# Layer 3 of the last batch: unpacked sign weights, one output per product, and the check of the sums moved ahead of its second half

## Chip, cores and metric

The kernel runs on one core of one Trainium2 chip. The metric is the device time of one execution in microseconds (us); lower is better. Times inside an execution are given from the start of the profiled span.

## What is computed

The input is `x`, 8 batches of 512 channels and 1024 (32 x 32) positions, in f32. Four layers follow each other:

- layer 0: three 1x1 convolutions to 64 channels, a batch norm over all batches for two of them, an attention without softmax that is divided by the largest singular value, a 1x1 convolution back to 512 channels, and a residual;
- layer 1: a group norm, an attention over 1024 positions with 512 channels and softmax, a projection, and a residual;
- layer 2: an attention over 1024 positions with 128 channels and softmax, a projection to 512 channels with a scale (`bn`), and a residual;
- layer 3, which the change touches:

```python
a = jnp.sign(x + c(rsign_bias))
scale = jnp.mean(jnp.abs(W), axis=1)
Wb = jnp.sign(W) * scale[:, None]
y = jnp.einsum('bchw,oc->bohw', a, Wb)
bn = c(bn_gamma) * (y - c(bn_mean)) * jax.lax.rsqrt(c(bn_var) + BN_EPS) + c(bn_beta)
s = bn + x
t = s - c(pr_shift)
out = jnp.where(t > 0, t, c(pr_slope) * t) + c(pr_bias)
```

Its product has only signs on both sides, so every sum of it is a whole number of at most 512 in size.

## The kernel before, in words

**Stages.** An opening stage loads the weights and all batches once, makes layer 0's projections and statistics, and folds weight products together. After it the main stage calls `fast` (line 768) once for each batch, in the order 6, 7, 0, 1, 2, 3, 4, 5. A last part reads one number, `bad`, and computes everything again on a general path if it isn't zero (lines 1444 and 1445). In the runs shown it is zero, so that path is skipped by a branch.

**One batch in `fast`.** The scores of layer 1 (`scores1`) and its values (`make_v`, `values1`, line 519) are block products of the Strassen kind: seven products where eight would be usual, with sums and differences of the blocks on VectorE. Then come layer 2's projections (`project2`, line 611), its scores (`scores2`), and its values (`values2`, L826). The 1024 positions are two halves of 512. Each half of layer 2 is closed by `close2` (line 646): four f32 products with the weights `z` (L650), added to the batch `xt` on VectorE (L652). An f32 product of 128x512 is two passes of TensorE in the trace. In the batches before the last, parts of the next batch's work (`make_u`, `split_h`) fill the gaps.

**Layer 3** is `leave` (line 654), a generator that does one half of the positions. ScalarE makes the signs of `xt` in f16 (L660, four instructions of 128x512, one per block of 128 channels). The sign weights lie packed in `sw3` (128 x 4 x 256, f16): one number holds two output channels, `lo + 1026 * hi`. A loop over `j` (0 and 1) makes four f16 products (L666) that accumulate into one PSUM bank; this bank holds two outputs' sums at once. They are taken apart in three steps: ScalarE divides by 1026 and adds a large constant, which rounds (L675); VectorE subtracts that constant (L676), which gives the upper sum; VectorE subtracts 1026 times the upper sum from the bank (L677), which gives the lower. For each of the two outputs of 128 channels there follow five more steps: a scale and the addition of `xt` on VectorE (L680), Relu (L684) and Identity (L685) on ScalarE, their combination on VectorE (L692), and the output transfer on SP's queue (L695).

**Where the halves of layer 3 stand.** The first half of a batch is done inside `fast` between the two `close2`. The second half is put on a list, `rest3`, and is done step by step beside the next batch's scores. The last batch has no next one, so its second half follows at once (lines 856 to 859) and with nothing beside it.

**The check of the sums.** For each batch and each attention `inverse_sums` (line 727) writes a few of the inverse softmax sums to the tile `guard` (64 rows x 2 x 128) by SP's queue (L745). After the last batch, nine small VectorE instructions (L1319 to L1329) see whether any is too large, too small, or differs too much between the halves. A product of one element on TensorE (L1331) counts the rows that fail, and VectorE copies the count to `bad` (L1332). `values_load` (L1444) then loads `bad` into a register on all five engines, and each engine branches on it (L1445). The end of the program (L1498) is a barrier of all engines.

**What sets the order.** The program is traced, and outside of a few hand-ordered TensorE passages of the opening stage a scheduler puts the instructions of each engine in order; waits between engines are semaphores. The order that the text speaks of is that of the built programs. Eight PSUM banks rotate under `bank` (line 121); the tiles `h`, `hs`, `us`, `uv` of the pool `big` have one buffer each, `small` has three, `e` eight.

Of the kernel before, what the change touches and what calls it, by code (L numbers as in the profile page):

```python
# [20 lines left out]
CC = C // P  # L21
# [62 lines left out]
def kernel(  # L84
# [36 lines left out]
    def bank():  # L121
        return psum["bank"].tile([P, HF], F32, tag="bank", name="bank")
# [16 lines left out]
    def half(i):  # L139
        return bass.ts(i, HF)  # L140
# [510 lines left out]
            xs = xt[:, oc, half(h)]  # L651
            nc.vector.tensor_tensor(xs, ps, xs, ALU.add)  # L652

    def leave(env, xt, dst, halves=range(NH)):

        small = env["small"]
        for h in halves:
            sg = env["e"].tile([P, CC, HF], F16, tag="e", name="sg")
            for cc in range(CC):
                nc.scalar.activation(  # L660
                    sg[:, cc, :], xt[:, cc, half(h)], AF.Sign, bias=rb3[:, cc : cc + 1]
                )
            for j in range(CC // 2):
                ps = bank()
                for cc in range(CC):
                    mm(  # L666
                        out=ps,
                        lhsT=sw3[:, cc, bass.ts(j, P)],
                        rhs=sg[:, cc, :],
                        start=cc == 0,  # L670
                        stop=cc == CC - 1,
                    )
                both = env["e"].tile([P, 2, HF], F32, tag="e", name="both")
                y1, y2 = both[:, 0, :], both[:, 1, :]
                nc.scalar.activation(y2, ps, AF.Identity, bias=round3, scale=1.0 / PACK)  # L675
                nc.vector.tensor_scalar(y2, y2, ROUND, None, ALU.subtract)  # L676
                nc.vector.scalar_tensor_tensor(y1, y2, -PACK, ps, ALU.mult, ALU.add)  # L677

                for y, oc in ((y1, j), (y2, j + 2)):
                    nc.vector.scalar_tensor_tensor(  # L680
                        y, y, sa3[:, oc : oc + 1], xt[:, oc, half(h)], ALU.mult, ALU.add
                    )
                    up = small.tile([P, HF], F32, tag="half_a", name="up3")
                    nc.scalar.activation(up, y, AF.Relu, bias=cb3[:, oc : oc + 1])  # L684
                    nc.scalar.activation(  # L685
                        y,
                        y,
                        AF.Identity,
                        bias=pb3[:, oc : oc + 1],
                        scale=col("L3_conv_pr_slope", oc),  # L690
                    )
# [4 lines left out]
                yield  # L696

    def channels(ap):
        return ap.rearrange("(cc p) n -> p cc n", p=P)
# [64 lines left out]
        return steps()  # L764

    rest3 = []

    def fast(env, n, hb, ua):
# [12 lines left out]

        es = [None] * NT
        for k, _ in enumerate(scores1(env, hb, ua, es)):
            if rest3 and k % 2:
                if next(rest3[0], "end") == "end":
                    rest3.pop()
                    if more and order[n + 1] not in resident:
                        resident[order[n + 1]] = load_x(order[n + 1])
            if k == 8 and more:
                ahead = entering(n + 1)  # L790
            if k >= 11 and k % 3 == 0:
                next(ahead, None)
# [12 lines left out]
        steps = iter(())  # L805
        for k, _ in enumerate(values1(env, xt, vt, es, r, scratch)):
            chore(2)
            if k == 5 and more:
                nxt = resident[order[n + 1]]
                hb = split_h(env, normal(env, nxt))  # L810
        if more:
            steps = make_u(env, hb, got)

        def fill(k=1):
            for _ in range(k):
                next(steps, None)

        tt, pt, gt = project2(env, xt, lambda h: fill(1 - h))
        es, esum = scores2(env, pt, tt, lambda t: fill(t % 2))
        banks, r = [None, None], None  # L820

        def values2(h, ts):
            if banks[h] is None:
                banks[h] = bank()
            for t in ts:
                mm(  # L826
                    out=banks[h],
                    lhsT=gt[:, t, :],
                    rhs=es[t][:, half(h)],
                    start=t == 0,  # L830
                    stop=t == NT - 1,
                )
# [14 lines left out]
        close2(xt, att, 0)  # L847
        att = values2(1, range(NTH, NT))
        fill()
        for _ in leave(env, xt, dst, [0]):  # L850
            fill()
        close2(xt, att, 1)
        fill(2)
        for _ in steps:
            pass
        rest3.append(leave(env, xt, dst, [1]))
        if not more:
            for _ in rest3.pop():
                pass

        return hb, got[0] if more else None
# [437 lines left out]
    with ExitStack() as main:  # L1299
        psum_pools(main, 0, 8)  # L1300
        big = main.enter_context(tc.tile_pool(name="big", bufs=1, reuse_waits="tile"))
        epool = main.enter_context(tc.tile_pool(name="epool", bufs=EBUFS))
        small = main.enter_context(tc.tile_pool(name="small", bufs=3))
        env.update({"big": big, "e": epool, "small": small})
        got = []
        hb = split_h(env, normal(env, resident[order[0]], True))
        for _ in make_u(env, hb, got):
            pass
        ua = got[0]
        for n in range(B):  # L1310
            hb, ua = fast(env, n, hb, ua)

        g = 2 * B * 4
        fine = small.tile([g, NH, P], F32, tag="half_a", name="fine")
        other = small.tile([g, NH, P], F32, tag="half_b", name="other")
        nbad = small.tile([g, 1], F32, tag="nbad", name="nbad")
        nc.vector.tensor_scalar(fine, guard, 1.0 / GUARD, None, ALU.is_gt)  # L1319
        nc.vector.tensor_scalar(other, guard, GUARD, None, ALU.is_lt)  # L1320
        nc.vector.tensor_tensor(fine, fine, other, ALU.mult)
        for h in range(NH):
            one = slice(0, g // 2)
            nc.vector.scalar_tensor_tensor(
                other[one, h, :], guard[one, 1 - h, :], RATIO, guard[one, h, :], ALU.mult, ALU.is_gt
            )
            nc.vector.tensor_tensor(fine[one, h, :], fine[one, h, :], other[one, h, :], ALU.mult)
        nc.vector.tensor_reduce(nbad, fine.rearrange("p h n -> p (h n)"), AX.X, ALU.min)
        nc.vector.tensor_scalar(nbad, nbad, -1.0, 1.0, ALU.mult, ALU.add)  # L1329
        ps = bank()  # L1330
        mm(out=ps[0:1, 0:1], lhsT=nbad, rhs=ones2[0:g, 0:1], start=True, stop=True)  # L1331
        nc.vector.tensor_copy(bad, ps[0:1, 0:1])  # L1332


    def attention(env, scores, scale, apply):

        at = None
# [107 lines left out]
    with tc.If(again > 0):  # L1445
        with (
            ExitStack() as stack,
            tc.tile_pool(name="gbig", bufs=1) as big,
# [53 lines left out]
```

## Time and profile before

| | us |
|---|---|
| three runs | 2003.36, 2006.15, 2007.2 |
| median | 2006.15 |
| profiled execution | 2006.29 |
| its span | 2004.5 |

The profile has five engines: PE is TensorE's matrix products, PEld its weight loads, DVE is VectorE, ACT is ScalarE, POOL is GpSimd; SP only issues transfers here. A letter q after an engine's name means its sequencer or queue. "bank<-sg,sw" means that an instruction writes `bank` from `sg` and `sw`; L666 is line 666. In the chain of work each row is a start, a length and what ran, and a row "issue" is time in which the engine waited for nothing that the profile shows.

The costliest groups of the page, with instructions, busy time and mean duration of one:

| line | engine | what | count | busy us | mean ns |
|---|---|---|---|---|---|
| L536 | PE | values of layer 1, 128x512 f32 | 768 | 334.0 | 593 |
| L369 | PE | scores of layer 1, 128x512 f32 | 384 | 183.3 | 598 |
| L826 | PE | values of layer 2, 128x512 f32 | 256 | 114.6 | 595 |
| L710 | PE | scores of layer 2, 128x512 f32 | 256 | 114.6 | 592 |

Rows of the kinds that the change touches, from the groups and from the views of single lines (128x512 unless another size is given):

| line | engine | what | ns |
|---|---|---|---|
| L666 | PE | f16 product, at full clock / at most | 379 / 634 |
| L650 | PE | f32 pass | 592 |
| L660 | ACT | signs | 717 |
| L675 | ACT | rounding step, from PSUM | 685 |
| L684, L685 | ACT | Relu, Identity | 716, 798 |
| L676 | DVE | subtraction of the constant | 423 |
| L677 | DVE | lower sum, from PSUM | 683 |
| L680, L692 | DVE | scale and add, combine | 744, 739 |
| L652 | DVE | close of layer 2, from PSUM | 679 |
| L1005 | DVE | packing of the signs, 128x1024 f16, once | 1218 |

The duration of a product is longer than its spacing: eight products of L666 stand at 1974.48 to 1976.37, one every 0.216 us.

### The profile page before, as it was taken

The numbers are of one execution on the slowest core, as the hardware profiler recorded it, in microseconds if no ns is written. First come the engines' busy times: TensorE is split into PE (matmuls) and PEld (weight loads), VectorE is DVE, ScalarE is ACT, GpSimd is POOL, SyncE is SP. The second block draws the span as 40 slices with busy tenths as digits, with TensorE's granted clock in tenths as the row PEclk, the third lists the DMA queues.
The fourth block names the chain that finished last, engine by engine and source line by source line (L and its number), as shares of the span: only waits on it lengthen the run. The fifth ranks groups of instructions, "written<-read, shape, count | busy, mean of one in ns | idle before, by whom it ended". The sixth has DMA issues, their size and how long they took to land.

```text
span 2004.5 us, 16625 instructions
## 1 busy us (share of the span) xinstructions
PE 1935.0 (97%) x6246; PEld 996.0 (50%) x6246; DVE 1113.0 (56%) x1827; ACT 539.0 (27%) x842; POOL 187.9 (9%) x152
## 2 busy tenths in 40 slices
PE   8999899999999999999999999999999999999995
PEld 2377346544465446454465446444645445544652
DVE  3245577337863586536752677248653675266435
ACT  2132222134221432124211332034202421233014
POOL 0000001100011000200011001100120011101110
PEclk9989999999999999999999999999999999999997
DMA  8320000002000020001100010002000200010001
GB/s 330 126 74 1 5 6 11 1 11 84 10 7 0 21 74 17 0 0 43 57 11 1 32 69 11 0 11 84 11 0 1 77 29 0 0 32 21 11 1 54
DMA packets 26711, 66.99 MB, mean 33 GB/s; under 512 B 3760, under 2 KB 4016, under 8 KB 25984
## 3 DMA queue, kind: packets, MB, share of 16 engines
q1 hardware_dynamic: 25968, 65.09, 9.5%
q8 instruction: 51, 0.84, 0.2%
q0 software_dynamic: 224, 0.33, 0.1%
q10 hardware_dynamic: 432, 0.43, 0.1%
q14 instruction: 36, 0.29, 0.0%
HBM read 38.51 MB, written 18.87 MB: 29 GB/s over the span
## 4 chain that ended last, share of the span: by engine, by line
PE 92%; DVE 4%; ACT 3%; issue 0%; DMA 0%; DVEq 0%; ACTq 0%
PE bank L369 36%; PE bank L536 19%; PE bank L826 6%; PE bank L621 5%; PE bank L710 5%; PE bank L1073 4%; PE bank L633 3%; PE bank L650 3%; PE bank L392 2%; PE bank L666 1%; PE bank L876 1%; PE wide L1129 1%; PE bank L1183 1%; PE bank L877 1%; PE bank L731 1%; DVE e L326 1%
## 5 line engine op out<-in xcount | busy, mean ns | idle before, releaser
L536 PE MATMUL bank<-e,vt 128*128 128x512 f32 x768 | 334.0, 593 | 0.0
L536 PEld LDWEIGHTS bank<-e,vt 128*128 128x128 f32 x768 | 145.0, 190 | 175.4 <-issue 171.7
L369 PE MATMUL bank<-ut,h 128*128 128x512 f32 x384 | 183.3, 598 | 4.7 <-ACT e L331 4.7
L369 PE MATMUL bank<-us,hs 128*128 128x512 f32 x256 | 121.3, 596 | 0.5 <-DVE us L298 0.5
L326 DVE TENSOR_TENSOR e<-bank,e 128x512 f32<-128x512 f32 x128 | 87.6, 684 | 61.3 <-PE bank L369 60.0
L826 PE MATMUL bank<-e,tpg 128*128 128x512 f32 x256 | 114.6, 595 | 0.0
L710 PE MATMUL bank<-tpg 128*128 128x512 f32 x256 | 114.6, 592 | 0.0
L369 PEld LDWEIGHTS bank<-ut,h 128*128 128x128 f32 x384 | 70.6, 190 | 87.7 <-issue 73.5
L621 PE MATMUL bank<-xt,tpg 128*128 128x512 f32 x256 | 113.6, 592 | 0.0
L369 PE MATMUL bank<-wo,h 128*128 128x256 f32 x384 | 95.7, 389 | 18.3 <-ACT vt L331 18.3
L717 ACT ACTIVATE e<-bank 128x512 f32<-128x512 f32 x128 | 76.4, 597 | 88.2 <-PE bank L710 88.2
L369 PE MATMUL bank<-h,wu 128*128 128x512 f32 x192 | 92.1, 603 | 3.4 <-DVE h L442 3.4
L326 DVE TENSOR_TENSOR vt<-bank,vt 128x512 f32<-128x512 f32 x64 | 44.0, 687 | 90.2 <-PE bank L369 89.3
L341 POOL TENSOR_TENSOR ut<-ut 128x512 f32<-128x512 f32 x16 | 21.8, 1360 | 733.9 <-ACT ut L322 733.9
L722 DVE TENSOR_TENSOR esum<-esum,e 128x1024 f32<-128x1024 f32 x48 | 58.8, 1226 | 54.8 <-ACT e L717 54.8
L369 PEld LDWEIGHTS bank<-wo,h 128*128 128x128 f32 x384 | 72.4, 193 | 31.0 <-ACT vt L331 21.5
L341 POOL TENSOR_TENSOR e<-e 128x512 f32<-128x512 f32 x32 | 41.6, 1301 | 441.1 <-ACT e L320 370.2
L826 PEld LDWEIGHTS bank<-e,tpg 128*128 128x128 f32 x256 | 48.0, 190 | 63.9 <-issue 63.9
L710 PEld LDWEIGHTS bank<-tpg 128*128 128x128 f32 x256 | 48.6, 190 | 60.8 <-issue 58.6
L621 PEld LDWEIGHTS bank<-xt,tpg 128*128 128x128 f32 x256 | 47.9, 190 | 56.4 <-issue 55.0
L369 PEld LDWEIGHTS bank<-us,hs 128*128 128x128 f32 x256 | 47.3, 190 | 57.5 <-issue 51.4
L660 ACT ACTIVATE sg<-xt,rb 128x512 f16<-128x512 f32 x64 | 43.7, 717 | 103.4 <-DVE xt L652 100.7
(300 smaller groups left out, 2995.9 us busy)
## 6 DMA issues: line engine op xcount, KB each, us to landing
xt<-in_x SPq DMA_DIRECT2D x56, 512.0 KB
out<-both SPq DMA_DIRECT2D x64, 256.0 KB
rfull<-rsum SPq DMA_DIRECT2D x64, 128.0 KB
f_dram<-f SPq DMA_DIRECT2D x8, 256.0 KB
fb<-f_dram SPq DMA_DIRECT2D x8, 256.0 KB
w<-in_w SPq DMA_DIRECT2D x1, 1024.0 KB
q<-in_w_q SPq DMA_DIRECT2D x1, 1024.0 KB
k<-in_w_k SPq DMA_DIRECT2D x1, 1024.0 KB
```

The source lines that it names most:

```text
L326: nc.vector.tensor_tensor(dst, ps, u, ALU.add)
L341: nc.gpsimd.tensor_tensor(c22, c22, c12, ALU.add)
L369: mm(out=ps[:, q * w : (q + 1) * w], lhsT=lt(ka, kb, q, k), rhs=rhs(ka, kb, q, k), start=first and q == 0 and k == 0, stop=last and k == 1 ...
L536: mm(out=ps, lhsT=a[:, t, bass.ts(r_, P)], rhs=e[t], start=first and t == 0, stop=last and t == NTH - 1, skip_group_check=True,)
L621: mm(out=ps, lhsT=sbw["tpg"][:, cc, bass.ts(i, P)], rhs=xt[:, cc, half(h)], start=cc == 0, stop=cc == CC - 1,)
L633: mm(out=ps[:, i, :], lhsT=xt[:, cc, bass.ts(4 * h + i, P)], rhs=sbw["tpg"][:, cc, 2 * P : 3 * P], start=cc == 0, stop=cc == CC - 1,)
L650: mm(out=ps, lhsT=sbw["z"][:, bass.ts(oc, P)], rhs=att, start=True, stop=True)
L710: mm(out=ps, lhsT=pt[:, 0, bass.ts(t, P)], rhs=tt[:, 0, half(h)], start=True, stop=True,)
L717: nc.scalar.activation(e[:, half(h)], ps, AF.Exp, scale=float(P) ** -0.5)
L722: nc.vector.tensor_tensor(esum, esum, e, ALU.add)
L826: mm(out=banks[h], lhsT=gt[:, t, :], rhs=es[t][:, half(h)], start=t == 0, stop=t == NT - 1,)
L1073: mm(out=banks[i][side(h), :], lhsT=w0[i][:, cc, :], rhs=xt[:, cc, half(h)], start=cc == 0, stop=cc == CC - 1,)
```

## The change

For the last batch only, `unpacked` makes two tiles of plain signs, `lo` and `hi` (f16, in the buffer of the tag `h`), out of `sw3`, with the same arithmetic that took the sums apart: three VectorE instructions of 128x1024. `leave` gets them as `signs` and then makes two products per `j`, one with `lo` and one with `hi`, each into its own bank; the three steps that took the sums apart are left out, and the scale and addition reads the bank. All other batches use `leave` as before.

The nine small instructions of the check, the product that counts, the copy to `bad` and the load of `bad` on all engines are now a function, `count_bad`, that is called after the last batch's second `close2` and before its second half of layer 3. Its three tiles come from the pool `late`, outside the main stage's pools. The branch stays at the end.

```diff
-    def leave(env, xt, dst, halves=range(NH)):
+    def leave(env, xt, dst, halves=range(NH), signs=None):
...
-                ps = bank()
-                for cc in range(CC):
-                    mm(
-                        out=ps,
-                        lhsT=sw3[:, cc, bass.ts(j, P)],
-                        rhs=sg[:, cc, :],
-                        start=cc == 0,
-                        stop=cc == CC - 1,
-                    )
                 both = env["e"].tile([P, 2, HF], F32, tag="e", name="both")
                 y1, y2 = both[:, 0, :], both[:, 1, :]
-                nc.scalar.activation(y2, ps, AF.Identity, bias=round3, scale=1.0 / PACK)
-                nc.vector.tensor_scalar(y2, y2, ROUND, None, ALU.subtract)
-                nc.vector.scalar_tensor_tensor(y1, y2, -PACK, ps, ALU.mult, ALU.add)
-
-                for y, oc in ((y1, j), (y2, j + 2)):
+
+                def product(lt):
+                    ps = bank()
+                    for cc in range(CC):
+                        mm(
+                            out=ps,
+                            lhsT=lt[:, cc, bass.ts(j, P)],
+                            rhs=sg[:, cc, :],
...
+                if signs is None:
+                    ps = product(sw3)
+                    nc.scalar.activation(y2, ps, AF.Identity, bias=round3, scale=1.0 / PACK)
+                    nc.vector.tensor_scalar(y2, y2, ROUND, None, ALU.subtract)
+                    nc.vector.scalar_tensor_tensor(y1, y2, -PACK, ps, ALU.mult, ALU.add)
+                    sums = y1, y2
+                else:
+                    sums = [product(lt) for lt in signs]
+
+                for y, ps, oc in ((y1, sums[0], j), (y2, sums[1], j + 2)):
                     nc.vector.scalar_tensor_tensor(
-                        y, y, sa3[:, oc : oc + 1], xt[:, oc, half(h)], ALU.mult, ALU.add
+                        y, ps, sa3[:, oc : oc + 1], xt[:, oc, half(h)], ALU.mult, ALU.add
                     )
...
+    def unpacked(env):
+
+        t = env["big"].tile([P, 2 * CC, N], F16, tag="h", name="signs")
+        lo, hi = (t[:, i].rearrange("p (cc c) -> p cc c", c=C // 2) for i in range(2))
+        near = env["big"].tile([P, 6, HF], F32, tag="hs", name="near")
+        near = near[:, 0:2, :].rearrange("p i (cc c) -> p (i cc) c", c=C // 2)
+        nc.vector.tensor_scalar(near, sw3, 1.0 / PACK, ROUND, ALU.mult, ALU.add)
+        nc.vector.tensor_scalar(hi, near, ROUND, None, ALU.subtract)
+        nc.vector.scalar_tensor_tensor(lo, hi, -PACK, sw3, ALU.mult, ALU.add)
+        return lo, hi
+
+    def count_bad(env):
...
+        g = 2 * B * 4
+        fine = late.tile([g, NH, P], F32, tag="fine", name="fine")
+        other = late.tile([g, NH, P], F32, tag="other", name="other")
+        nbad = late.tile([g, 1], F32, tag="nbad", name="nbad")
...
+        nc.vector.tensor_copy(bad, ps[0:1, 0:1])
+        return nc.values_load(bad, min_val=0, max_val=P)
...
+        signs = None
         if more:
             steps = make_u(env, hb, got)
+        else:
+            signs = unpacked(env)
...
-        for _ in leave(env, xt, dst, [0]):
+        for _ in leave(env, xt, dst, [0], signs):
             fill()
...
-        rest3.append(leave(env, xt, dst, [1]))
+        rest3.append(leave(env, xt, dst, [1], signs))
         if not more:
+            verdict.append(count_bad(env))
             for _ in rest3.pop():
                 pass
...
-    again = nc.values_load(bad, min_val=0, max_val=P)
-    with tc.If(again > 0):
+    with tc.If(verdict[0] > 0):
```

The lines that compute the check were taken out of the end of the main stage unchanged, but for the pool of their tiles. In the changed kernel the products of layer 3 have line 670, the scale and addition 689, Relu and Identity 693 and 694, the combination 701, the output transfer 704, the unpacking 713 to 715, the check 726 to 739, the load of `bad` 740 and the branch 1472.

More of the change, by code (lines that the diff above doesn't have):

```diff
@@ L663, in leave @@
             for j in range(CC // 2):
[L664 to L672 removed]
                 both = env["e"].tile([P, 2, HF], F32, tag="e", name="both")
                 y1, y2 = both[:, 0, :], both[:, 1, :]
[L675 to L679 removed]
+                def product(lt):
[5 more added lines that the diff above has]
+                            rhs=sg[:, cc, :],
+                            start=cc == 0,
+                            stop=cc == CC - 1,
+                        )
+                    return ps
+                if signs is None:
[7 more added lines that the diff above has]
+                for y, ps, oc in ((y1, sums[0], j), (y2, sums[1], j + 2)):
                     nc.vector.scalar_tensor_tensor(
[L681 removed]
+                        y, ps, sa3[:, oc : oc + 1], xt[:, oc, half(h)], ALU.mult, ALU.add
                     )
@@ L696, in leave @@
                 yield
+    def unpacked(env):
[12 more added lines that the diff above has]
+        nbad = late.tile([g, 1], F32, tag="nbad", name="nbad")
+        nc.vector.tensor_scalar(fine, guard, 1.0 / GUARD, None, ALU.is_gt)
+        nc.vector.tensor_scalar(other, guard, GUARD, None, ALU.is_lt)
+        nc.vector.tensor_tensor(fine, fine, other, ALU.mult)
+        for h in range(NH):
+            one = slice(0, g // 2)
+            nc.vector.scalar_tensor_tensor(
+                other[one, h, :], guard[one, 1 - h, :], RATIO, guard[one, h, :], ALU.mult, ALU.is_gt
+            )
+            nc.vector.tensor_tensor(fine[one, h, :], fine[one, h, :], other[one, h, :], ALU.mult)
+        nc.vector.tensor_reduce(nbad, fine.rearrange("p h n -> p (h n)"), AX.X, ALU.min)
+        nc.vector.tensor_scalar(nbad, nbad, -1.0, 1.0, ALU.mult, ALU.add)
+        ps = bank()
+        mm(out=ps[0:1, 0:1], lhsT=nbad, rhs=ones2[0:g, 0:1], start=True, stop=True)
+        nc.vector.tensor_copy(bad, ps[0:1, 0:1])
+        return nc.values_load(bad, min_val=0, max_val=P)
     def channels(ap):
@@ L766 @@
     rest3 = []
+    verdict = []
     def fast(env, n, hb, ua):
@@ L1311 @@
             hb, ua = fast(env, n, hb, ua)
[L1315 to L1332, printed above, removed]
     def attention(env, scores, scale, apply):
```

## Prediction

> **What bounds the kernel now.** I read the page first: its engine shares and the chain that ended last. The columns of the first line are busy time, share of the span and instructions.
>
> ```profile
> PE 1935.0 (97%) x6246; PEld 996.0 (50%) x6246; DVE 1113.0 (56%) x1827; ACT 539.0 (27%) x842; POOL 187.9 (9%) x152
> ...
> PE 92%; DVE 4%; ACT 3%; issue 0%; DMA 0%; DVEq 0%; ACTq 0%
> ```
>
> TensorE bounds seven and a half batches, and nothing before the last batch's values changes on any engine. So I went to the stage after the last f32 products: the same chain in order of time (start, us, what), from 1900 us on.
>
> ```profile
> 1971.21 3.43 PE bank L826 x8
> 1974.64 0.88 PE bank L666 x4
> ...
> 1985.82 1.45 PE bank L666 x3
> 1987.27 0.02 issue
> 1987.30 0.70 ACT both L675
> 1987.99 0.02 issue
> 1988.02 0.44 DVE both L676
> ...
> 1996.61 0.20 DVE fine L1327
> ...
> 1998.23 0.15 DVE bad L1332
> ```
>
> After 1975.5 TensorE is on the chain only for single products: ScalarE and VectorE carry it, the check of the sums stands last, and 6.1 us pass between its end (1998.38) and the end of the span (2004.5) without any busy instruction. The source view of the branch on the check (line 1445) shows what is in them: engine, operation, count, duration min/median/max, first and last start.
>
> ```profile
> L1445 PEldq COMPARE_BRANCH  x1: 4239/4239/4239, 1999.1 to 1999.1; - x1
> L1445 DVEq COMPARE_BRANCH  x1: 72/72/72, 1999.2 to 1999.2; - x1
> ...
> L1445 ACTq EVENT_SEMAPHORE  x1: 17/17/17, 2001.9 to 2001.9; - x1
> L1445 DVEq EVENT_SEMAPHORE  x1: 21/21/21, 2002.6 to 2002.6; - x1
> L1445 PEldq EVENT_SEMAPHORE  x1: 51/51/51, 2003.4 to 2003.4; - x1
> ```
>
> Every engine loads `bad`, branches, and reaches its next instruction only 2.9 us (ACT), 3.3 us (DVE) and 4.4 us (PE) later. PE's is last and sets the end, 1.1 us after it. The windows view gives the clock (us, busy by engine, PEclk, DMA share, GB/s):
>
> ```profile
> 1968.00:1976.00 8.00, 8.00 (x24) 3.45 (x23) 3.65 (x6) 3.34 (x5) 0.00 (x0) 1.00 0.00 0
> ...
> 1982.00:1988.00 6.00, 3.89 (x8) 0.91 (x7) 4.03 (x7) 5.09 (x9) 0.00 (x0) 0.51 0.45 175
> ```
>
> **What the skill says.** "TensorE: Matmul & The Clock Gate", Part 1, has the array at half clock after an idle window of about 3.4 us and at full clock after a busy one. The trace agrees: TensorE idled 2.77 us before 1982.57, the clock is 0.51 from 1982, and the f16 product goes from 379 to 634 ns. "Runtime: NRT & Kernel Launch", "Instruction fetch mechanics", says that a taken branch to code outside the fetched window waits for a DMA; the 2.9 to 4.4 us above fit. "Perfetto Trace Analysis", "Per-engine timelines", lets a sequencer go on once an instruction is pushed into the wait queue. Here it doesn't run past an unmet wait: DVE's waits of line 1444 begin at 1998.2, with the copy of `bad`, and not earlier.
>
> **The change, part by part.** The sum is made against the profiled span, 2004.5 us (its execution took 2006.29; the three runs 2003.36, 2006.15, 2007.2). I worked it with the order in which the changed program's instructions stand on each engine, each instruction starting when its engine is free or its last input is there, with the durations of this trace. Times are from the span's start.
>
> Unpacking: three VectorE instructions of 128x1024, once, beside L558 and L559 of the last batch. No row shows f16 into f32. Nearest are L442 (128x1024 tensor-scalar, 0.80 us) and L1005 (128x1024 scalar-tensor-tensor, 1.22): 0.80 + 0.80 + 1.22 = 2.8 us; ends 2.1 (if f16 runs at twice L442's pace) and 3.7 (three at 1.22). Two of them stand ahead of L559, which so ends at 1878.5 instead of 1876.9. TensorE needs that result only after four groups of 8 passes at 0.43 us, at 1887.2, and the next VectorE results (L567, L569, done by 1882.3) at 1894.0. Cost 0, at either end, hidden under the products of lines 536; it can't be a gain, since TensorE has no idle time there.
>
> First half of layer 3: 16 products instead of 8. At full clock they follow each other at 0.216 us (8 took from 1974.48 to 1976.21), so +1.73 us on TensorE, and the second half's close (L650, 8 passes of 0.43 us) runs from 1977.9 to 1981.5 instead of 1976.2 to 1979.8. What is removed are L675 (0.69), L676 (0.43) and L677 (0.69) twice, the work that kept VectorE from L652: its first L652 of this half started at 1979.59 with its input long there. Now it starts at 1979.3. The six L652 and output steps between go on at 0.60 to 0.67 us each and end at 1984.0 instead of 1985.4; the last sign ends at 1984.8 instead of 1986.4. Gain 1.6.
>
> Check moved up: nine small VectorE instructions (0.15 to 0.42 us, together 2.6, with their dependent starts some 3.0) stand among the first half's L652, ahead of the second `att`. VectorE idled 0.17 + 0.24 + 0.17 + 2.67 = 3.25 us there, until 1974.68, so `att` isn't later; the four signs end at 1972.7, before TensorE asks at 1974.48. The first of them waits for the `guard` transfers; their issues end at 1967.1 and no packet moves after 1968, while VectorE comes there at 1969.3. Cost 0; the bound is 0.3 us on `att`, with no effect before 1977.9, when L650 needs it. The product of `bad` is behind the close on TensorE, its copy at 1984.0 on VectorE. SP's load of `bad` (0.49, with two register steps 0.7) is now queued ahead of the last four output transfers; it runs at about 1984.1, and the first of those is due at 1988.7. Cost 0. PE's, ACT's and VectorE's own loads remain behind their last work; POOL has none left.
>
> Second half, to the first output: TensorE has done ten products when the last sign comes at 1984.8; one more and the first sum is there at 1985.2. VectorE scales it from PSUM (L677's row 0.69, L680's 0.74; I take 0.74), and ScalarE starts its first Relu at 1986.05. Before it was 1990.20, through L675, L676, L677 and L680. Gain 4.15, of which 1.6 was counted. From there ScalarE bounds: four Relus (0.72) and four Identities (0.80) in the new order, two of which wait for their predecessor. That makes 5.8 us against the 5.5 of before; ScalarE ends at 1991.83 instead of 1995.70. TensorE's last product ends at 1986.3 and is not in the way. The last VectorE instruction starts at 1991.9 instead of 1995.87: gain 4.0.
>
> The end: the last output instruction started 8.63 us before the end. 1.06 us of the check stood between outputs, and 1.8 behind the last. Now VectorE's four waits, load and branch take 1.02 us from the start of its last instruction (1998.23 to 1999.25), its fetch 3.3, and the closing barrier 1.1: 5.4 us; I take 5.3, as PE's and POOL's fetches no longer run beside it. PE's branch starts near 1986.9 and is over by 1991.3. The last transfer's landing was signalled 2.0 us after its data was ready (1998.62 after 1996.61); that makes 1994.6 now, and SP, whose 16 further waits take 0.066 us each, is at the barrier by 1995.7, ahead of VectorE (1996.2). Gain 3.3.
>
> Sum: 4.0 + 3.3 = 7.3 us. 2006.15 - 7.3 = **1998.85 us**, a span near 1997.2.
>
> **The rivals.** (a) *Clock*: TensorE works 77% of 1981.6 to 1986.3, in three bursts, and the window's place in time isn't set by the kernel. If the clock halves at 1982.15 as before, products follow at 0.427 us: after the second sign they queue, and the first sum comes at 1986.66 instead of 1985.22. +1.4: 2000.3. For it: it halved there before. Against it: the window of 1978.7 to 1982.15 had 31% TensorE work before and has 82% now.
> (b) *The end stays whole*: if 6.1 us still follow the last output (another engine's fetch becomes the late one), 1992.6 + 6.1 = 1998.7, a gain of 5.8: 2000.3. With (a): 2001.7.
> (c) *Load ahead*: if VectorE's load and branch run while its last outputs wait, its fetch is hidden and SP sets the end: 1995.7 and the 1.1 of the barrier are 0.4 us earlier than the forecast's span: 1998.4. Against it stands the start of its waits at 1998.2.
> (d) *Slower*: the doubled products run at half clock. If it falls before the last values of `att` (L826, 1971.9), six passes cost 2.6 more, the first half's 16 products 3.4, the close 3.4 and the second half 1.4: 10.8, less 7.3. One window earlier adds 1.7: +5.2, 2011.3. It decides from a fall before about 1974. Against it: TensorE has no gap there, and has 1.00 in 1968 to 1976.
> (e) *It does not do what it says*: the products or the check stand serially after all and nothing is gained, 2006. The order on the engines speaks against it.
>
> **How the numbers follow.** Forecast 0.64; (a) 0.11; (b) 0.13; (c) 0.07; (d) 0.02; (e) 0.03. The range goes down to 1996.0, the forecast less the 2.8 us by which the lowest run lies below the median, which also covers (c), and up to 2002.3: (a) and (b) together, 2001.7, plus 0.6 for my schedule of VectorE and ScalarE. A measurement of this kernel tells about 0.2%, 4.0 us, from no change, that is below 2002.1. Faster 0.88: all of the forecast, (c), and most of (a) and (b); same 0.09; slower 0.03.
>
> **What would show it.** Right: 32 f16 products of line 670 at the end, at 379 ns and clock 1.00 until about 1986; the first Relu of the second half near 1986.1; L701's last start near 1992; the copy of `bad` near 1984; PE's branch early, and VectorE's semaphore step the last before the barrier. Wrong: idle time of TensorE in L536, a clock of 0.5 from 1982 on, or a VectorE gap of over 0.3 us at the check's first instruction.

## The result, and the profile after

| | before | after |
|---|---|---|
| runs | 6 | 6 |
| median, us | 2005.87 | 1999.28 |
| lowest to highest, us | 2003.36 to 2007.2 | 1998.48 to 2003.85 |
| profiled span, us | 2004.5 | 1997.5 |
| first f16 product of the last batch's layer 3 to the end, us | 30.03 | 22.77 |

The medians differ by 6.6 us, and the forecast was 1998.85. The ratio is 0.9972, with a 95% interval of 0.9959 to 0.9984: faster, by 3.2 to 8.2 us. The last row is the one to work with. The same stages before the last batch's tail take up to 3.8 us more or less from one profile to the next (the first f16 product stood between 1971.4 and 1975.2 us in all profiles of this study), whatever the kernel does at its end. From that product on two profiles with the same tail agree to 0.03 us: 22.77 here, 22.80 in e6_unpack_x6. There is one profile of each kernel.

The page of the changed kernel, its engine shares and the chain that ended last, says as little as before: 16 more products on TensorE, five fewer instructions on VectorE, four fewer on ScalarE.

```profile
PE 1936.9 (97%) x6262; PEld 997.3 (50%) x6262; DVE 1111.1 (56%) x1822; ACT 536.6 (27%) x838; POOL 187.9 (9%) x152
...
PE 92%; DVE 4%; ACT 3%; issue 1%; DMA 0%; DVEq 0%; ACTq 0%
```

The chain in order of time (start, us, what), in the stage where the change is:

```profile
1974.93 2.60 PE bank L670 x12
...
1984.20 0.01 DVE bad L739
...
1985.01 0.39 PE bank L670
1985.40 0.02 issue
1985.42 0.76 DVE both L689
1986.18 0.02 issue
1986.21 0.73 ACT up L693
...
1991.05 0.82 ACT both L694
1991.88 0.02 issue
1991.90 0.75 DVE both L701
```

One product of 0.39 us follows the last sign, the scale and addition reads its bank, and the first Relu starts at 1986.21. Of the check only the copy to `bad` is on the chain, with 0.01 us ahead of the last sign; the chain ends with the last output. The clock stays whole over the stage where it was 0.51 (windows: us, busy by engine, PEclk, DMA share, GB/s):

```profile
1976.00:1982.00 6.00, 5.94 (x22) 2.58 (x20) 5.78 (x9) 5.29 (x8) 0.00 (x0) 1.00 0.14 53
1982.00:1988.00 6.00, 3.93 (x16) 1.44 (x15) 4.83 (x9) 4.52 (x8) 0.00 (x0) 1.00 0.32 124
```

And the source view of the branch, now line 1472 (engine, operation, count, duration, first and last start):

```profile
L1472 POOLq COMPARE_BRANCH  x1: 45/45/45, 1985.2 to 1985.2; - x1
L1472 PEldq COMPARE_BRANCH  x1: 3326/3326/3326, 1986.0 to 1986.0; - x1
L1472 PEldq EVENT_SEMAPHORE  x1: 51/51/51, 1989.4 to 1989.4; - x1
...
L1472 DVEq COMPARE_BRANCH  x1: 72/72/72, 1993.2 to 1993.2; - x1
...
L1472 DVEq EVENT_SEMAPHORE  x1: 21/21/21, 1996.4 to 1996.4; - x1
```

TensorE and GpSimd branch while the outputs are still being made, so the times until they go on (3.4 us on TensorE) cost nothing. VectorE, which has the last output, branches at 1993.2, is there again at 1996.4, and is the last; the end follows at 1997.5.

### The profile page after: what moved, and what is told of

Read it like the earlier page. It is cut to its first block, busy times and chain, and to the rows that moved or that the text cites. A ratio compares the mean times of both kernels' runs of the same rounds, so it can differ in the third digit from the quotient of the medians.

```text
span 1997.5 us, 16654 instructions
## 1 busy us (share of the span) xinstructions
PE 1936.9 (97%) x6262; PEld 997.3 (50%) x6262; DVE 1111.1 (56%) x1822; ACT 536.6 (27%) x838; POOL 187.9 (9%) x152
## 4 chain that ended last, share of the span: by engine, by line
PE 92%; DVE 4%; ACT 3%; issue 1%; DMA 0%; DVEq 0%; ACTq 0%
PE bank L369 37%; PE bank L536 19%; PE bank L874 6%; PE bank L621 6%; PE bank L754 6%; PE bank L1122 4%; PE bank L633 3%; PE bank L650 3%; PE bank L392 2%; PE bank L670 1%; PE bank L925 1%; PE wide L1178 1%; PE bank L1232 1%; PE bank L926 1%; PE bank L775 1%; DVE e L326 1%
## 5 line engine op out<-in xcount | busy, mean ns | idle before, releaser
L536 PE MATMUL bank<-e,vt 128*128 128x512 f32 x768 | 334.0, 593 | 0.0
L536 PEld LDWEIGHTS bank<-e,vt 128*128 128x128 f32 x768 | 145.0, 190 | 175.4 <-issue 171.7
```

The source lines that it names most:

```text
L536: mm(out=ps, lhsT=a[:, t, bass.ts(r_, P)], rhs=e[t], start=first and t == 0, stop=last and t == NTH - 1, skip_group_check=True,)
```

## The experiments

All times of this table are counted from the first f16 product of the last batch's layer 3, in the profiled execution. "Relu" is the first one of the second half, "output" the start of the last combination on VectorE.

| kernel | last sign ends | Relu | output | end | ratio, 95% interval |
|---|---|---|---|---|---|
| before | 11.90 | 15.72 | 21.39 | 30.03 | |
| after | 10.18 | 11.44 | 17.13 | 22.77 | 0.9972 [0.9959, 0.9984] |
| e1_signs_only | 10.19 | 11.64 | 17.52 | 25.78 | 0.9979 [0.9973, 0.9986] |
| e2_check_only | 11.90 | 15.72 | 21.26 | 26.95 | 0.9987 [0.9981, 0.9994] |
| e3_half2_only | 11.91 | 13.79 | 19.48 | 25.08 | 0.9976 [0.9968, 0.9984] |
| e4_half1_only | 10.19 | 13.55 | 19.09 | 24.83 | 0.9975 [0.9968, 0.9983] |
| e9_late_tiles | 10.18 | 11.63 | 17.33 | 22.81 | 0.9969 [0.9958, 0.998] |
| e10_small_tiles | 10.19 | 14.51 | 20.32 | 25.84 | one time, 2001.87 us |
| e6_unpack_x6 | 10.19 | 11.44 | 17.14 | 22.80 | one time, 1999.66 us |
| e8_no_branch | 10.18 | 11.63 | 17.33 | 21.38 | 0.9961 [0.9945, 0.9976] |
| e7_pool | 10.18 | 11.43 | 16.80 | 22.66 | 0.9964 [0.9952, 0.9976] |
| e11_pool_apart | 10.19 | 11.44 | 15.79 | 22.36 | 0.9963 [0.995, 0.9977] |
| e12_last_on_act | 10.19 | 11.44 | 15.80 | 22.28 | 0.9966 [0.9954, 0.9978] |
| e13_pool_no_branch | 10.18 | 11.63 | 15.99 | 20.07 | 0.9956 [0.994, 0.9973] |

### The two parts alone

e1_signs_only takes the check back to its old place and its old tiles:

```diff
-        fine = late.tile([g, NH, P], F32, tag="fine", name="fine")
...
+        fine = env["small"].tile([g, NH, P], F32, tag="half_a", name="fine")
...
-            verdict.append(count_bad(env))
...
             hb, ua = fast(env, n, hb, ua)
+        count_bad(env)
...
+    again = nc.values_load(bad, min_val=0, max_val=P)
+    with tc.If(again > 0):
```

> Unpacked signs for both halves of the last batch, but the check as before: its tiles from the pool small, its code after the main stage, the load of bad at the end. My theory (two gains that add up: 4.0 us from the signs, 3.3 us from the check): the last output instruction starts near 1991.9 as in the changed kernel, and 8.6 us follow it as before, so the span is near 2000.5, 4.0 us under before's (ratio 0.998) and 3.0 us over the changed kernel's. Rival (the end is set by the last output alone, the check fills time that would pass anyway): 5.6 us follow, a span near 1997.5, ratio 0.9965.

e2_check_only leaves `signs` at None in the last batch too, and keeps the rest.

> Signs packed in every batch as before, the check moved up as in the changed kernel. My theory: the last output instruction starts where it did before, 1995.8 to 1996.1, and 5.4 to 5.6 us follow it: a span of 2001.2 to 2001.7, about 3 us under before's (ratio 0.9985). Rival 1 (moving the check costs what it saves, because its nine small instructions hold up the first half's work on VectorE): the last output starts 1 us or more later, span 2002.5 or more. Rival 2 (the end stays 6.1 us whole): span 2002.7.

Measured: e1_signs_only gains 4.25 us (30.03 to 25.78), e2_check_only 3.08, together 7.33, against the 7.26 of the whole change: the two parts add up. In e1_signs_only 8.26 us follow the start of the last output, and TensorE's branch is the late one again. Its source view of the branch:

```profile
L1472 PEldq COMPARE_BRANCH  x1: 3938/3938/3938, 1995.3 to 1995.3; - x1
...
L1472 PEldq EVENT_SEMAPHORE  x1: 51/51/51, 1999.3 to 1999.3; - x1
```

In e2_check_only 5.69 us follow it instead of 8.63, and the output starts 0.13 us earlier. The rivals of both fall: the check does not fill time that would pass anyway, and it costs nothing where it stands now. One difference lies beside what these edits are for: in e1_signs_only, e8_no_branch, e9_late_tiles and e13_pool_no_branch twelve of the second half's products, not ten, stand on TensorE ahead of the first that needs the last sign, and the first Relu comes 0.2 us later than in the changed kernel.

### The two halves of layer 3

e3_half2_only and e4_half1_only each take one `signs` out of the two calls of `leave`:

```diff
-        for _ in leave(env, xt, dst, [0], signs):
+        for _ in leave(env, xt, dst, [0]):
```

> The changed kernel, but the last batch's first half of layer 3 uses the packed signs again (8 products and the three steps that take the sums apart); the second half and the check stay as changed. My theory (the first half's unpacking frees VectorE for the second half's close, and keeps TensorE busy): the last sign of the second half ends near 1986.5 instead of 1985.0, TensorE idles over 2 us before its first product of that half, and the clock halves near 1982 as before; the 16 products then queue, the first Relu of the second half starts near 1989.2, the last output near 1994.9, span near 2000.5 (ratio 0.998). If the clock holds: first Relu near 1987.7, span near 1999.1. Rival (the first half's part is useless, eight added products for nothing): the first Relu at 1986.2 or earlier, span 1997.5 or less.

> The changed kernel, but the last batch's second half of layer 3 uses the packed signs (8 products and the three steps that take the sums apart); the first half and the check stay as changed. Counted from the first f16 product of the last batch to the end of the span: before 30.0 us, the check alone moved 26.95, check and second half unpacked 25.08, everything 22.77. Theory (the halves' gains add up: the first half's is that VectorE reaches the second half's close earlier, 1.6 to 1.7 us, plus what the clock gives by staying full): the last sign ends 10.2 us after the first f16 product as in the changed kernel (11.9 with a packed first half), all products run at 379 ns, and 24.6 to 25.2 us pass to the end; ratio about 0.9978. Rival (the first half's part only matters through the clock, since the three steps of the second half wait for TensorE anyway): 26 us or more.

Measured against e2_check_only (26.95) and the changed kernel (22.77): the first half's unpacking is worth 2.12 us alone and 2.31 on top of the second's, the second half's 1.87 alone and 2.06 on top. e4_half1_only came as expected, with all products at up to 379 ns. e3_half2_only lies between its two cases, a half clock and a whole one. Windows of e3_half2_only:

```profile
1980.00:1982.00 2.00, 0.00 (x0) 0.00 (x0) 2.00 (x4) 2.00 (x4) 0.00 (x0) 1.00 0.00 0
1982.00:1984.00 2.00, 1.24 (x4) 0.40 (x4) 2.00 (x4) 2.00 (x4) 0.00 (x0) 0.81 0.69 262
1984.00:1986.00 2.00, 1.48 (x4) 0.56 (x4) 2.00 (x5) 2.00 (x4) 0.00 (x0) 0.50 0.34 131
1986.00:1988.00 2.00, 2.00 (x9) 0.78 (x7) 0.62 (x3) 0.40 (x1) 0.00 (x0) 0.83 0.34 131
```

TensorE stands still in the first window while VectorE and ScalarE are full, and the clock falls. From the means it fell at about 1983.24 (0.81 of two us) and was whole again at about 1986.68 (0.83): 3.4 us of half clock. Only six of the 16 products were slow (up to 634 ns). TensorE was busy for 2.72 of these 3.4 us; in the kernel before it was busy for 2.02 of the 3.42 us that follow the fall at 1982.15, and there the clock stayed at 0.50. That the share of work decides on the return is argued from such pairs. So the first half's unpacking does two things: the last sign comes 1.72 us earlier, and the products keep TensorE from standing still.

### What moved the check

e9_late_tiles has the check's code and the load where the kernel before has them, behind the main stage, and only its three tiles from the pool `late`. e10_small_tiles is the opposite: the code between the halves, the tiles from `small` as before.

> Unpacked signs as in the changed kernel; the check's code stands after the main stage as in the kernel before, and bad is loaded there, but its three tiles come from the pool late. Theory A (the tiles' buffers hold the check back, not its place in the text: half_a and half_b of the pool small are in use by the outputs): VectorE does the nine instructions in the same place as in the changed kernel, near 1969.6 to 1973.7, and span and ratio are the changed kernel's (1997.5, 0.9965; 22.8 us from the first f16 product of the last batch to the end). Theory B (the place in the text decides): the check is behind the last output, 8.6 us after its start, span near 2000.5, ratio 0.998.

> The changed kernel, but the check's three tiles come from the pool small (tags half_a, half_b, nbad) as in the kernel before, while its code stands between the halves as in the changed kernel. By the order of the built program VectorE then does the nine instructions after the second half's close and ahead of its first scale and addition, not among the first half's. Theory (work on VectorE there is on the path, the same work near 1970 is not): the copy of bad ends 3 us later than in the changed kernel, the first Relu of the second half starts 13.4 to 14.2 us after the first f16 product instead of 11.44, and 24.8 to 25.5 us pass from that product to the end instead of 22.77. Rival (VectorE's idle time before the first sum, 1.2 us, and the wait of ScalarE hide the check there too): 23.5 us or less.

Source view of the check's first instruction in e9_late_tiles, whose whole tail stands 1.3 us earlier than the changed kernel's:

```profile
L726 DVE TENSOR_SCALAR fine<-guard x1: 275/275/275, 1968.2 to 1968.2; 64x256 f32<-64x256 f32 x1
```

The code is traced last, and still runs in the first half; `bad` is copied at 1982.8, and 22.81 us to the end is the changed kernel's 22.77. Theory A holds: e1_signs_only differs from this kernel in the pool of the three tiles alone, and there the same instruction starts at 1991.1. With tiles from `late`, the place in the text moves nothing. Of the two tags it is `half_a`, in use by `up` of the outputs, that held the check back. In the kernel before, the one instruction that needs only the tile of `half_b` runs in the first half already (timeline):

```profile
1975.29 0.27 DVE L1320 TENSOR_SCALAR other<-guard 64x256 f32<-64x256 f32 x1
```

In e10_small_tiles the check, but for that one instruction, stands between the halves' work on VectorE: L726 starts at 1983.6. With tiles from `small` the place in the text does count, as e1_signs_only has the same tiles and runs L726 at 1991.1; I take it that the place decides which uses of `half_a` the check comes behind. It costs 3.07 us, 0.3 more than the most I expected. The chain shows why it is so dear:

```profile
1985.73 0.16 DVE nbad L736
1985.88 0.04 issue
1985.93 0.19 PE bank L738 x2
1986.11 1.84 PE bank L670 x4
1987.97 0.76 DVE both L689
```

The product that counts stands in TensorE's queue ahead of the second half's products. These wait for a check that has nothing to do with them, TensorE stands still, and the clock falls (six of the 16 products took 609 to 635 ns). The changed kernel has the same order on TensorE; there the check is done at 1973.7, long before.

### The slack behind the unpacking

e6_unpack_x6 does the three unpacking instructions six times over; the values are the same.

> The changed kernel with the three unpacking instructions done six times over, 13 us more on VectorE in the stage of layer 1's values of the last batch. Theory (TensorE bounds that stage and VectorE's work there has slack): no idle time of TensorE in L536, and from the first product of that stage's part that follows the unpacking (the 32 passes that begin at 1873.72 in the changed kernel) to the first f16 product of layer 3 it takes 101.05 us as in the changed kernel, within 0.1. Rival (VectorE's work there shows up in the end): up to 13 us more, a part of it in the waits for what VectorE computes behind it.

Eighteen instructions, 15.6 us in all, in the place of three of 2.6 us, and from the product at 1874.03 to the first f16 product pass 101.05 us, as in the changed kernel to 0.01 us. The theory holds. The scheduler spread the repeats among the other work, so what is shown is that VectorE has 13 us to spare there, not that a block of 13 us would be free.

### The end, and a faster version

e8_no_branch leaves out the general path, the load of `bad` and the branches. The others move two of the second half's four Identity steps to GpSimd; e7_pool writes over the input, e11_pool_apart to a tile of its own, e12_last_on_act issues the last transfer on ScalarE's queue, e13_pool_no_branch is e11_pool_apart without what e8_no_branch leaves out. From e11_pool_apart:

```diff
...
+                    z = y
+                    if signs and h and oc >= 2:
+                        z = small.tile([P, HF], F32, tag="half_b", name="line3")
+                        nc.gpsimd.tensor_scalar(
+                            z, y, col("L3_conv_pr_slope", oc), pb3[:, oc : oc + 1], ALU.mult, ALU.add
+                        )
+                    else:
...
-                        y, up, ps3[:, oc : oc + 1], y, ALU.mult, ALU.add
+                        y, up, ps3[:, oc : oc + 1], z, ALU.mult, ALU.add
```

> Leaves out the general path, the load of bad and the branch on all engines; the check's instructions and its count remain where the changed kernel has them. Theory (VectorE's load, branch and fetch after its last output, 4.3 us, set the end, but the landing of the last transfer stands close behind): the end moves to the landing, 2.0 to 2.3 us after the last output instruction's end, then SP's waits and the barrier of 1.1 us: 4.6 to 5.1 us after the start of the last output instead of 5.64, 21.8 to 22.3 us from the first f16 product to the end. Rival (the branch's fetch is the whole of it, nothing stands behind): 2.5 to 3.5 us after the start of the last output. Second rival (the fetch comes at the end of the program anyway): 5.6 us.

> The changed kernel, with one more edit: in the last batch's second half the Identity of the outputs with the upper sums (two of four) is done on GpSimd instead of ScalarE, with the same slope and bias, beside ScalarE's Relu. Theory (from the first Relu on ScalarE bounds the end, and GpSimd is free): GpSimd's instruction of 128x512 takes 0.9 to 1.4 us (its additions of that size took 1.27), ScalarE has 4.5 us instead of 5.8 to do, VectorE's last output starts 0.8 to 1.2 us earlier than 17.13 us after the first f16 product, and the span ends as much earlier: 21.6 to 22.0 us after that product instead of 22.77. Rival (GpSimd and VectorE hold each other up, GpSimd at 2.4 us as in its slowest rows): the last output is as late as before or later, 22.8 us or more.

> As e7_pool, but GpSimd writes its result to a tile of its own instead of over its input, so that it needn't wait until ScalarE's Relu has read that input. Theory (the wait for the Relu was what made e7_pool's second GpSimd instruction start 2.2 us late): GpSimd takes 0.9 us, starts right after the scale and addition, and is done before ScalarE's last Relu; ScalarE's 4.5 us then set the last output, which starts 15.9 to 16.2 us after the first f16 product (17.13 in the changed kernel, 16.80 in e7_pool); 5.6 to 5.9 us follow, so 21.6 to 22.0 us from that product to the end, ratio 0.9958 to 0.9962. Rival (GpSimd and VectorE hold each other up when they run beside each other): 16.8 or later.

> As e11_pool_apart, but the transfer of the very last output is issued on ScalarE's queue instead of SP's. In e11_pool_apart the last output starts 1.34 us earlier than in the changed kernel and the span ends only 0.41 us earlier: SP took 1.26 us to issue the last transfer instead of 0.33, and SP, not VectorE, reached the closing barrier last. Theory (the issue was held up by the transfers that SP had put on its own queue shortly before): ScalarE's issue takes 0.35 to 0.5 us, the landing is signalled 0.8 to 1.2 us earlier than in e11_pool_apart (20.24 us after the first f16 product), VectorE's fetch sets the end again, 21.4 to 21.8 us after that product instead of 22.36. Rival (what holds the issue up is common to all queues, such as the transfers of instructions after the branches): an issue of 1 us or more on ScalarE too, and 22.3 us or more.

> As e11_pool_apart, but the general path, the load of bad and the branches are left out, as in e8_no_branch. In e11_pool_apart and e12_last_on_act the last transfer's 16 parts (one for each of the core's 16 DMA engines) signalled up to 1.6 us apart, the last of them 3.6 us after the start of the issue; in e8_no_branch they signalled within 0.14 us, 2.5 us after it. Theory (transfers of instructions that follow the branches occupy one of these engines, and the output's part on it waits behind them): without branches the last parts signal within 0.3 us of each other, and 4.0 to 4.3 us pass from the start of the last output to the end as in e8_no_branch, 19.8 to 20.1 us from the first f16 product to the end. Rival (the outputs hold each other up, because two of them now follow each other 0.7 us apart): still over 0.8 us apart, and 20.6 us or more.

e8_no_branch: 4.06 us follow the start of the last output. That is under my case (4.6 to 5.1) and over the rival's (2.5 to 3.5): the landing of the last transfer does stand behind the branch, but further behind: the branches cost 1.58 us of the changed kernel's 5.64, where I had expected 0.5 to 1.0 (1.39 from the first product to the end, as the output starts 0.2 us later).

e7_pool gained 0.33 us of output, a miss, by my edit: GpSimd overwrote what Relu was still to read, so its second instruction started only at 1987.3, after the last Relu. With a tile of its own (e11_pool_apart) the output starts 1.34 us earlier than in the changed kernel, 0.1 more than expected, but the end only 0.41. The wait moved to SP: it took 1.26 us to issue the last transfer, and 3.7 us passed from there until SP saw it landed, against 2.25 in the changed kernel. So I tried ScalarE's queue. Source view of the output transfer in e12_last_on_act:

```profile
L712 SPq DMA_DIRECT2D out<-both x63: 332/333/350, 461.0 to 1989.7; - x63
...
L712 ACTq DMA_DIRECT2D out<-both x1: 363/363/363, 1990.4 to 1990.4; - x1
```

The issue is short, 0.36 us, as the theory had it, and yet the landing takes 3.6 us again, and the end stays at 22.28. My theory about the landing falls, and why SP's issue took 1.26 us stays open. The theory also left out that ScalarE's own load and branch now come behind the issue: ScalarE goes on only at 1994.75, so with the 1.1 us of the barrier an early landing could have brought no less than 22.0. The Trainium skill, "DMA: Bandwidth & Descriptors", "Issuing engines are not separate DMA queues", would have told me: transfers of all issuing engines run on the same 16 DMA engines. "Why a DMA increments its semaphore by 16 and not by 1" says where to look next: every DMA engine adds one when its part is written. The semaphore records of e12_last_on_act have 13 of the last transfer's 16 steps by 1992.52, and the others at 1992.89, 1993.30 and 1994.02. In e8_no_branch all 16 lie within 0.14 us. The DMA view over the last 8 us (queue and kind, packets, MB, share) has a kind of transfer in e11_pool_apart

```profile
q1 hardware_dynamic: 576, 1.05, 34.5%
q14 instruction: 5, 0.04, 1.5%
q8 instruction: 1, 0.02, 1.5%
```

that isn't there in e13_pool_no_branch, whose last 8 us have nothing but the outputs:

```profile
q1 hardware_dynamic: 576, 1.05, 34.3%
```

These are the fetches that the branches cause; the one of 16 KB starts at 1989.92 in e11_pool_apart and takes 1.86 us, beside the outputs. Without them (e13_pool_no_branch) the last 16 steps lie within 0.15 us, the landing is 2.0 us after the start of the issue, the issue takes 0.33 us, and 4.08 us follow the last output: the theory of that run holds, and the rival (outputs 0.7 us apart hold each other up) falls. Without the branches GpSimd's part brings 1.31 us (21.38 to 20.07), with them 0.41. That the late parts are those of the DMA engine that fetches is argued from the times; the records of the packets do not name the engine, and the runs without branches have no load of `bad` either. It fits that in e12_last_on_act the last eight packets of the last output start one by one, every 0.08 us from 1992.94 on, right behind the last of the output before.

e11_pool_apart and e12_last_on_act end 0.4 to 0.5 us earlier than the changed kernel in the profile; the intervals of their ratios overlap with its own, so the times alone don't rank them.

## Why the prediction was right

Counted from the first f16 product, it had 7.3 us to gain; 7.26 were gained. The spans differ by 0.29 less, as the tail began 0.29 us later in the profile of after. That the two numbers are so close is in part luck: the output came 0.3 us earlier than forecast and the end behind it took 0.3 us longer. The runs' times alone (3.2 to 8.2 us) can't tell such parts apart; the profiles do.

- **Unpacking, at nothing.** Right. It took 0.68 + 0.69 + 1.22 = 2.6 us (estimate 2.8; its lower end should read 2.0, by 0.40 + 0.40 + 1.22), L559 ended at 1878.1 (1878.5), TensorE has no gap in L536, and six times the work changes nothing either.
- **Output 4.0 us earlier.** 4.26. The first Relu stands 11.44 us after the first product instead of 15.72, 0.13 us earlier than forecast, and ScalarE needed 5.66 us from there instead of 5.8 (the eight durations that the forecast names sum to 6.1, but ScalarE's instructions overlap: two Relus in a row take 1.32 us). As a sum it was right, its split wasn't: I put 1.6 on the first half, and the runs show 2.1 to 2.3; the second half has 1.9 to 2.1 instead of 2.4. The sign came 1.72 us earlier (1.6), and what the full clock gives belongs to the first half, whose products keep TensorE at work: with the first half packed, it halves (e2_check_only, e3_half2_only); with it unpacked, it doesn't (e1_signs_only, e4_half1_only), unless the check stands in TensorE's way (e10_small_tiles).
- **Check moved, at nothing.** Right: L726 at 1969.57, the last of the nine ended at 1973.7, the four signs were done at 1973.1, before the first product at 1974.77. What I took as given is the cause: the pool of the tiles gave this order. The place in the text alone would have given that of e10_small_tiles, and 3 us more.
- **The end, 3.3 us.** 2.99. VectorE's fetch (3.2 us, forecast as 3.3 less 0.1) and the barrier (1.1) were as worked out; the load of `bad` took 0.82 us instead of 0.54, which is the missing 0.3. The last transfer landed at 1994.92 instead of 1994.6; SP was at its wait for VectorE by 1995.93, and waited 0.52 us there, so VectorE set the end, as forecast. The reading that every engine goes on only some 3 us after its branch was too wide: in the kernel before, SP went on after 0.5 us and GpSimd after 0.2.
- **Rival (a), the clock**, did not come: it stayed 1.00 until the products were done, and fell at about 1989.25. In all ten profiles with an unpacked first half and the check out of TensorE's way it stayed whole until the last product. That is not luck of the window's place: counted from the first product, the clock fell at 7.7 us in the kernel before, at 8.8 in e3_half2_only and at 9.2 in e2_check_only, and at 14.5 in the changed kernel, 15.6 in e1_signs_only and 16.1 in e8_no_branch, each 6.8 to 6.9 us later, that is two stretches of the 3.4 us that e3_half2_only was slow. The places are the same, and the packing of the first half decides. The stretch ahead of a fall need not be idle, though: in the kernel before TensorE was busy for 1.06 of its 3.41 us. **(b)**, the end whole, falls with TensorE's branch at 1986.0, over by 1989.4 (forecast 1986.9 and 1991.3). **(c)**, VectorE's load ahead of its outputs, falls with the load at 1992.3. **(d)** and **(e)** fall with the windows and the chain.

## What to carry to other kernels

A short piece of work at the end of a program can be held back by the buffers it is given and not only by where it is written: before moving code, look at who holds its tiles, and let a scheduler do the rest. Work that costs nothing in one place can cost its whole length a few us later, and what stands in a queue behind it pays too; so ask for the engine's idle time at that place, and not for its share of the span. When the last thing in a program is a branch, let the engines that are done early take it early, and count with the transfers of instructions that run beside the last outputs.

## What I had not expected of the hardware

- With branches shortly before it, single parts of an output transfer came late: the 16 parts lay up to 1.6 us apart in e12_last_on_act, 0.15 us without branches. That the transfers of instructions do it is argued.
- A load of one number into a register is not constant: on VectorE 0.54 us in the kernel before, 0.82 in the changed one, 0.58 in e11_pool_apart. The runs don't show why.
- A branch with its fetch holds TensorE for 4.24 us when all engines branch at once (3.94 in e1_signs_only), and for 3.3 to 3.8 when it branches ahead of the others.
- GpSimd's instruction of 128x512 took 0.76 and 1.78 us in e11_pool_apart, the longer one beside VectorE's combinations, which read two operands from SBUF. The Trainium skill, "SBUF — State Buffer", "Who interferes with whom", has such a VectorE instruction and a GpSimd read wait for each other; the two times fit that.
